# Attention on one core: the exponentials of four heads in one tile and one addition a step; copies and the next image's norm on ScalarE; the projection's matmuls together

## The chip, the cores and the metric

The kernel runs on one core of a Trainium2 chip. The metric is the device time of one execution in microseconds (us), given as the median of several runs, lowest and highest behind it. In the profiles PE is TensorE's matmuls, PEld its weight loads (they overlap PE), DVE is VectorE, ACT is ScalarE, POOL is GpSimd.

## The reference, cut to what matters

Everything is fp32; the input has four images of 256 channels and 48 by 48 pixels. Two layers follow one another. The first holds the part that the change touches:

```python
# layer 0: x = x + conv_layer(group_norm(x)), of which:
q, k, v = (qkv[:, :, :d], qkv[:, :, d:2 * d], qkv[:, :, 2 * d:])      # 8 heads of d = 32, N = 2304
attn = softmax(einsum('bhdn,bhdm->bhnm', q, k) * scale, axis=-1)
out = einsum('bhem,bhnm->bhen', v, attn).reshape(B, C, H, W)
out = einsum('oc,bchw->bohw', proj_w, out) + proj_b[None, :, None, None]
# layer 1: dynamic filters on group_norm(x), [cut]
```

## The kernel before

Each image goes through convolution and qkv, attention with projection, and the filter stage. Attention works in ten units for an image: two groups of four heads by five columns of queries (four of 512, one of 256). A unit has 18 steps, one for each 128 keys. `scores` of a step makes four products on TensorE and two exponentials on ScalarE, each over a pair of heads. `weigh` of the step before multiplies the exponentials by the values into `num` and lets VectorE add them into `acc`; the softmax sums come from `acc` over the partitions, with matmuls by ones, one for each head, at the end (`close`). Step 8 skips VectorE and goes straight into that sum.

```python
def scores(u, m):
    # [cut: four matmuls into ss[0], ss[1], two heads each]
    ps = []
    for pair in range(2):
        p = work0.tile([P, 2, QC], F32, tag=f"p{pair}", name=f"p_{b}_{u}_{m}_{pair}", bufs=3)
        nc.scalar.activation(p[:, :, :n], ss[pair][:, :, :n], AF.Exp, scale=QS)
        ps.append(p)
    return ps

def weigh(u, m, ps):
    # [cut: num, acc made at m == 0; four matmuls num[r] += vT, ps[j // 2][:, j % 2]]
    if m in DIRECT:                       # DIRECT = (8,)
        # [cut] sums(u, the four heads of ps, ...)
    elif m == 0:
        st["first"] = ps
    else:
        for pair in range(2):
            a = st["acc"][:, 2 * pair : 2 * pair + 2, :n]
            other = st["first"][pair][:, :, :n] if m == 1 else a
            nc.vector.tensor_tensor(a, other, ps[pair][:, :, :n], ALU.add)
    if m == NT - 1:
        st["out"] = work0.tile([P, QC], F32, tag="out", name=f"no_{b}_{u}")
        nc.vector.tensor_copy(st["out"][:, :n], st["num"][:, :n])

for i, (u, m) in enumerate(steps):
    ps = scores(u, m)
    if prev is not None:
        weigh(*steps[i - 1], prev)
    prev = ps
    if m == 2 and u:
        close(u - 1)                      # sums over partitions, 1/sum, ao = out * that
    if m == 6 and u % NH == 0:            # NH = 2: a finished column of 384 goes to the projection
        while (chunk + 1) * CH <= units[u][1]:
            project(chunk, ao, ps2(f"pp_{b}_{chunk}"))
            chunk += 1
    if m > 4 and u > 1 and spare:         # pieces of the next image's norm, one a step
        spare.pop(0)(ps_a)

def project(b, c, ao, pp, norm):
    for o in range(NH):
        for g in range(NH):
            nc.tensor.matmul(pp[:, o, :CH], wp[:, g, o * P : (o + 1) * P],
                             ao[:, g, c * CH : (c + 1) * CH], start=(g == 0), stop=(g == NH - 1))
        x1 = inside(t, o, c * R, R)
        nc.vector.scalar_tensor_tensor(out=x1, in0=rows_of(pp[:, o, :CH]), ...)   # + bias + x
        norm.part(o, c, x1)               # statistics, on VectorE
        # [cut: store of x1]
```

The projection thus alternates matmuls of one output half with VectorE's reading of that half, from one tile `pp` whose buffers are shared with the scores.

## Time and profile before

| | before |
|---|---|
| time, us | 3422.59 (3419.55 to 3422.88, three runs) |
| span of the profiled run, granted clock | 3419.3 us, 0.963 |
| PE, DVE, ACT busy, share of the span | 92%, 70%, 43% |
| attention, from first to last scores, images 0 to 3 | 414.3, 414.8, 418.4, 406.9 us |

The prediction shows the stages, the ring of the steps and the two places where TensorE waits for VectorE. Beside them, these are the groups of instructions that the change edits. A line reads: source line, engine, operation, output and inputs, their shapes, count, then busy time, mean ns of one, then idle time of the engine just before these instructions and what ended most of it.

```profile
L721 ACT ACTIVATE p<-se 128x1024 f32<-128x1024 f32 (+1 forms) x1440 | 1273.6, 937 | 377.2 <-PE se L709 341.0
L754 DVE TENSOR_TENSOR acc<-acc,p 128x1024 f32<-128x1024 f32 (+1 forms) x1200 | 1250.5, 1112 | 42.0 <-ACT p L721 41.1
```

Next the timeline, in which equal instructions that follow closely are one line: start, length, engine, line, tiles, count.

```profile
261.69 34.14 DVE L754 TENSOR_TENSOR acc<-acc,p 128x1024 f32<-128x1024 f32 x30
```

The table of waits (waiting engine and tile, waited-for engine and tile, then us in all, times, longest) also has:

```profile
PE num L737 <- DVE no L757: 35.4, 32, 3.3
PEld den L761 <- DVE acc L754: 1.8, 4, 0.5
```

The first is the copy that holds TensorE at the end of units. The second says that closing sums, which need the last addition, hardly wait.

### The profile page before, as it was taken

Reading aid. Unit: us, or ns where it says so; the run is one execution under the profiler, and the core shown is the slowest. Engines: PE = TensorE matmul, PEld = TensorE weight load, DVE = VectorE, ACT = ScalarE, POOL = GpSimd, SP = SyncE. Lnnn points to the kernel's source line nnn. Section 1 sums busy time; section 2 is a strip of 40 time slices with the busy share of each in tenths; the row PEclk is TensorE's granted clock in tenths of the full one; section 3 lists DMA queues with packets and bytes.
Section 4 is the critical chain, followed back from the end, with each engine's and each line's share of the span. In section 5 each row is a group of like instructions: output and inputs, shape, how many; then the busy total and the mean of one; then the engine's idle time right before and its main releaser. Section 6 shows DMA issues by size and latency. Waiting matters only on the chain. (4 is left out here: it accounts for less than half of the span.)

```text
span 3419.3 us, 45333 instructions
## 1 busy us (share of the span) xinstructions
PE 3158.2 (92%) x17814; PEld 1363.3 (40%) x17814; DVE 2377.3 (70%) x2837; ACT 1471.5 (43%) x1739; POOL 1041.5 (30%) x793
## 2 busy tenths in 40 slices
PE   7999999999989999999998999999998999987873
PEld 4542222445652222345563222245565222233442
DVE  2059899455659898836557899955555999876655
ACT  0067777300118777600024777730011887750002
POOL 0000000068770000037783000007786000007994
PEclk9999999999999999999999999999999999998876
DMA  3110000000002000000003000000000100022004
GB/s 119 29 27 6 6 10 6 15 24 5 10 14 52 6 6 10 11 28 10 5 10 61 6 6 10 6 6 5 5 10 16 23 6 6 10 81 100 10 5 176
DMA packets 70973, 81.52 MB, mean 24 GB/s; under 512 B 51280, under 2 KB 62048, under 8 KB 67680
## 3 DMA queue, kind: packets, MB, share of 16 engines
q1 hardware_dynamic: 69952, 73.15, 7.5%
q0 software_dynamic: 800, 5.41, 0.4%
q8 instruction: 141, 2.31, 0.3%
q14 instruction: 80, 0.66, 0.1%
HBM read 50.23 MB, written 28.31 MB: 23 GB/s over the span
## 5 line engine op out<-in xcount | busy, mean ns | idle before, releaser
L1060 POOL TENSOR_TENSOR cat<-cat,prod 128x768 f32<-128x768 f32 (+7 forms) x768 | 1034.1, 1352 | 2330.1 <-DVE prod L1058 2288.0
L721 ACT ACTIVATE p<-se 128x1024 f32<-128x1024 f32 (+1 forms) x1440 | 1273.6, 937 | 377.2 <-PE se L709 341.0
L754 DVE TENSOR_TENSOR acc<-acc,p 128x1024 f32<-128x1024 f32 (+1 forms) x1200 | 1250.5, 1112 | 42.0 <-ACT p L721 41.1
L709 PE MATMUL se<-q,k 32*128 32x512 f32 (+1 forms) x5760 | 830.5, 602 | 15.8 <-ACT p L721 12.6
L1058 DVE TENSOR_TENSOR prod<-wb,pad 128x768 f32<-128x768 f32 (+7 forms) x768 | 560.5, 750 | 404.4 <-PE wb L1035 369.8
L737 PE MATMUL num<-p,vT 128*32 128x512 f32 (+1 forms) x5760 | 716.6, 568 | 35.4 <-DVE no L757 35.4
L631 PE MATMUL pc<-pad,wc 128*128 128x384 f32 x1728 | 624.1, 494 | 2.3 <-issue 2.3
L1035 PE MATMUL wb<-w,pick 90*128 90x384 f32 (+3 forms) x888 | 478.7, 563 | 58.6 <-DVE prod L1058 52.2
L709 PEld LDWEIGHTS se<-q,k 32*128 32x128 f32 x5760 | 285.1, 184 | 565.2 <-issue 452.7
L631 PEld LDWEIGHTS pc<-pad,wc 128*128 128x128 f32 x1728 | 317.7, 191 | 219.1 <-issue 47.7
L990 PE MATMUL py<-cat,wsc 128*128 128x384 f32 x960 | 365.9, 511 | 16.7 <-POOL cat L1060 16.7
L737 PEld LDWEIGHTS num<-p,vT 128*32 128x32 f32 x5760 | 114.8, 108 | 529.5 <-issue 464.2
L640 ACT ACTIVATE hid<-pc,bn_t_f,bn_s_f 128x384 f32<-128x384 f32 x48 | 32.2, 672 | 614.5 <-PE pc L631 614.5
L1035 PEld LDWEIGHTS wb<-w,pick 90*128 90x128 f32 x888 | 172.3, 197 | 220.2 <-DVE prod L1058 101.6
L990 PEld LDWEIGHTS py<-cat,wsc 128*128 128x128 f32 x960 | 187.2, 200 | 127.4 <-POOL cat L1060 22.9
L875 PE MATMUL pg<-pad,wcat 128*45 128x384 f32 x864 | 173.1, 514 | 2.5 <-DVE pad L585 2.2
L1050 DVE TENSOR_TENSOR cat<-wb,pad 128x768 f32<-128x768 f32 x120 | 114.6, 955 | 86.9 <-PE wb L1035 86.3
L1005 ACT COPY y<-py 128x768 f32<-128x768 f32 x24 | 19.2, 799 | 317.4 <-PE py L990 317.4
L651 PE MATMUL pq<-hid,wqkv 128*128 128x384 f32 x384 | 135.0, 486 | 0.0
L679 DVE TENSOR_REDUCE qm<-q 128x1 f32<-128x2304 f32 x8 | 20.4, 2546 | 156.6 <-ACT q L658 156.5
L812 PE MATMUL pp<-ao,wp 128*128 128x384 f32 x192 | 82.2, 559 | 38.0 <-DVE pad L820 37.1
L754 DVE TENSOR_TENSOR acc<-p,p 128x1024 f32<-128x1024 f32 (+1 forms) x80 | 85.8, 1115 | 32.2 <-ACT p L721 32.2
(115 smaller groups left out, 1085.1 us busy)
## 6 DMA issues: line engine op xcount, KB each, us to landing
pad<-in_x SPq DMA_DIRECT2D x14, 1152.0 KB, 14.7
x_d<-pad SPq DMA_DIRECT2D x48, 192.0 KB, 2.5
y_d<-y SPq DMA_DIRECT2D x24, 384.0 KB, 2.7
xst<-in_x SPq DMA_DIRECT2D x18, 384.0 KB, 3.9
y<-y_d SPq DMA_DIRECT2D x3, 2304.0 KB, 19.6
out<-y SPq DMA_DIRECT2D x6, 1152.0 KB, 12.6
x<-x_d SPq DMA_DIRECT2D x2, 2304.0 KB, 24.2
x_first<-in_x SPq DMA_DIRECT2D x2, 1152.0 KB, 7.3
```

The source lines that it names most:

```text
L631: nc.tensor.matmul(pc[:, :CH], wc[:, i, k, o * P : (o + 1) * P], window(gn, i, c * R, k // 3 - 1, k % 3 - 1), start=(i == 0 and k == 0), s ...
L651: nc.tensor.matmul(pq[:, :CH], wqkv[:, i, s, g * P : (g + 1) * P], hid[:, i, cols], start=(i == 0), stop=(i == NH - 1),)
L709: nc.tensor.matmul(ss[j // 2][:, j % 2, :n], k_[r, g, m * P : (m + 1) * P], q[r, g, q0 : q0 + n], start=True, stop=True,)
L721: nc.scalar.activation(p[:, :, :n], ss[pair][:, :, :n], AF.Exp, scale=QS)
L737: nc.tensor.matmul(st["num"][r, :n], vT[:, m, g * P + j * D : g * P + (j + 1) * D], ps[j // 2][:, j % 2, :n], start=(m == 0), stop=(m == N ...
L754: nc.vector.tensor_tensor(a, other, ps[pair][:, :, :n], ALU.add)
L875: nc.tensor.matmul(pg[64 * s : 64 * s + NG, :CH], wcat[:, i, k, :], window(gn, i, (c + s) * R, k // 3 - 1, k % 3 - 1), start=(i == 0 and k ...
L990: nc.tensor.matmul(py[c][:, o, :CH], wsc[:, n * NH + i, o * P : (o + 1) * P], rhs(i), start=(n == 0 and i == 0), stop=(n == len(DILATIONS) ...
L1035: nc.tensor.matmul(pw[:, : nr * WW], pick[:, k : k + 1].to_broadcast([2 * NG, P]), w[:, l0 * WW : l1 * WW], start=True, stop=True,)
L1050: nc.vector.tensor_tensor(accv, wb, src, ALU.mult)
L1058: nc.vector.tensor_tensor(pv, wb, src, ALU.mult)
L1060: nc.gpsimd.tensor_tensor(dst, dst, pv, ALU.add)
```

## The change

The intent: fewer instructions on VectorE (one addition of 2048 elements a step instead of two of 1024), two kinds of work moved from VectorE to ScalarE (the copy of `num`, the normalising of the next image), and a projection whose eight matmuls run through before VectorE's reading is needed.

```diff
@@ Norm.finish
                 self.mean, self.rstd = mean, rstd
+                self.shift = small.tile([P, NH], F32, tag="gshift", name=f"gshift_{self.name}")
+                nc.vector.scalar_tensor_tensor(
+                    out=self.shift, in0=mean, scalar=-1.0, in1=rstd, op0=ALU.mult, op1=ALU.mult
+                )
@@ scores
-                ps = []
+                p = work0.tile([P, 4, QC], F32, tag="p", name=f"p_{b}_{u}_{m}", bufs=3)
                 for pair in range(2):
-                    p = work0.tile(
-                        [P, 2, QC], F32, tag=f"p{pair}", name=f"p_{b}_{u}_{m}_{pair}", bufs=3
-                    )
-                    nc.scalar.activation(p[:, :, :n], ss[pair][:, :, :n], AF.Exp, scale=QS)
-                    ps.append(p)
-                return ps
+                    nc.scalar.activation(
+                        p[:, 2 * pair : 2 * pair + 2, :n], ss[pair][:, :, :n], AF.Exp, scale=QS
+                    )
+                return p
@@ weigh (the matmuls and sums() take p[:, j] instead of ps[j // 2][:, j % 2]; cut)
-                    for pair in range(2):
-                        a = st["acc"][:, 2 * pair : 2 * pair + 2, :n]
-                        other = st["first"][pair][:, :, :n] if m == 1 else a
-                        nc.vector.tensor_tensor(a, other, ps[pair][:, :, :n], ALU.add)
+                    a = st["acc"][:, :, :n]
+                    other = st["first"][:, :, :n] if m == 1 else a
+                    nc.vector.tensor_tensor(a, other, p[:, :, :n], ALU.add)
                 if m == NT - 1:
                     st["out"] = work0.tile([P, QC], F32, tag="out", name=f"no_{b}_{u}")
-                    nc.vector.tensor_copy(st["out"][:, :n], st["num"][:, :n])
+                    nc.scalar.copy(st["out"][:, :n], st["num"][:, :n])
@@ project
                         stop=(g == NH - 1),
                     )
+            for o in range(NH):
                 x1 = inside(t, o, c * R, R)
@@ piece of the next image's norm
-                    return lambda ps_a: normalize(t, t, nn.mean, nn.rstd, h)
+                    return lambda ps_a: nc.scalar.activation(
+                        t, t, AF.Identity, bias=nn.shift[:, h : h + 1], scale=nn.rstd[:, h : h + 1]
+                    )
```

More of the change, by code (lines that the diff above doesn't have):

```diff
@@ L715, in scores, with weigh @@
                     )
-                ps = []
+                p = work0.tile([P, 4, QC], F32, tag="p", name=f"p_{b}_{u}_{m}", bufs=3)
                 for pair in range(2):
-                    p = work0.tile(
-                        [P, 2, QC], F32, tag=f"p{pair}", name=f"p_{b}_{u}_{m}_{pair}", bufs=3
-                    )
-                    nc.scalar.activation(p[:, :, :n], ss[pair][:, :, :n], AF.Exp, scale=QS)
-                    ps.append(p)
-                return ps
+                    nc.scalar.activation(
+                        p[:, 2 * pair : 2 * pair + 2, :n], ss[pair][:, :, :n], AF.Exp, scale=QS
+                    )
+                return p
             state = {}
-            def weigh(u, m, ps):
+            def weigh(u, m, p):
                 g, q0 = units[u]
@@ L739, in weigh @@
                         vT[:, m, g * P + j * D : g * P + (j + 1) * D],
-                        ps[j // 2][:, j % 2, :n],
+                        p[:, j, :n],
                         start=(m == 0),
@@ L746, in weigh @@
                         st["den"] = ps_a.tile([P, 512], F32, tag="den", name=f"den_{b}_{u}")
-                    sums(u, [p[:, jj, :n] for p in ps for jj in range(2)], m == DIRECT[0], False)
+                    sums(u, p[:, :, :n], m == DIRECT[0], False)
                 elif m == 0:
-                    st["first"] = ps
+                    st["first"] = p
                 else:
-                    for pair in range(2):
-                        a = st["acc"][:, 2 * pair : 2 * pair + 2, :n]
-                        other = st["first"][pair][:, :, :n] if m == 1 else a
-                        nc.vector.tensor_tensor(a, other, ps[pair][:, :, :n], ALU.add)
+                    a = st["acc"][:, :, :n]
+                    other = st["first"][:, :, :n] if m == 1 else a
+                    nc.vector.tensor_tensor(a, other, p[:, :, :n], ALU.add)
                 if m == NT - 1:
                     st["out"] = work0.tile([P, QC], F32, tag="out", name=f"no_{b}_{u}")
-                    nc.vector.tensor_copy(st["out"][:, :n], st["num"][:, :n])
+                    nc.scalar.copy(st["out"][:, :n], st["num"][:, :n])
             def sums(u, rhs, start, stop):
+                n = rhs.shape[2]
                 for j, r in enumerate(heads):
-                    nc.tensor.matmul(state[u]["den"][r, : rhs[j].shape[1]], ones, rhs[j],
+                    nc.tensor.matmul(state[u]["den"][r, :n], ones, rhs[:, j, :],
                                      start=start, stop=stop)
@@ L768, in close @@
                 st = state[u]
-                sums(u, [st["acc"][:, j, :n] for j in range(4)], False, True)
+                sums(u, st["acc"][:, :, :n], False, True)
                 t = work0.tile([P, QC], F32, tag="rden", name=f"rt_{b}_{u}", bufs=1)
```

## The prediction

> **What bounds the kernel now.** I read the page first (busy shares, then the costliest groups), then the busy time of each engine by stage, then the timeline of single steps, then the table of who waits for whom. The kernel has four images, each with an attention stage and a stage of dynamic filters. The change touches attention and the projection that hangs on it. Busy time by stage, first attention of images 0 to 3, then their filter stages; columns are the stretch, its length, then PE, PEld, DVE, ACT and POOL busy, granted clock, DMA share and GB/s:
>
> ```profile
> 212.80:629.70 416.90, 395.95 (x3078) 113.78 (x3079) 376.91 (x410) 321.19 (x364) 0.00 (x0) 0.98 0.03 6
> 1022.00:1441.50 419.50, 397.46 (x3089) 114.10 (x3086) 377.61 (x412) 321.12 (x363) 0.00 (x0) 0.98 0.09 18
> 1836.00:2258.50 422.50, 400.40 (x3085) 115.29 (x3080) 377.20 (x411) 321.20 (x363) 0.00 (x0) 0.98 0.09 18
> 2646.00:3057.00 411.00, 393.46 (x3078) 112.55 (x3072) 371.34 (x391) 319.74 (x361) 0.00 (x0) 0.99 0.06 13
> ```
>
> Attention is 1670 us of 3419, and no engine fills it alone: PE 95%, VectorE 90%, ScalarE 77%. That asks for the timeline. One attention is 10 units (two head groups by five query columns, the last of 256 instead of 512), each of 18 steps. Steady steps, then the end of unit 1, of image 0:
>
> ```profile
> 286.97 1.94 ACT L721 ACTIVATE p<-se 128x1024 f32<-128x1024 f32 x2 [0.19 <-PE se L709]
> 286.98 1.06 PE L737 MATMUL num<-p,vT 128*32 128x512 f32 x8
> ...
> 287.97 1.20 PE L709 MATMUL se<-q,k 32*128 32x512 f32 x8
> ...
> 289.10 1.06 PE L737 MATMUL num<-p,vT 128*32 128x512 f32 x8
> ...
> 289.15 1.94 ACT L721 ACTIVATE p<-se 128x1024 f32<-128x1024 f32 x2 [0.24 <-PE se L709]
> ...
> 295.58 1.94 ACT L721 ACTIVATE p<-se 128x1024 f32<-128x1024 f32 x2 [0.18 <-PE se L709]
> 295.75 0.68 DVE L757 COPY no<-num 128x512 f32<-128x512 f32 x1
> ...
> 296.49 1.07 PE L737 MATMUL num<-p,vT 128*32 128x512 f32 x8 [0.83 <-DVE no L757]
> ```
>
> The reader is to see a ring. Two exponentials take 1.94 us, 0.19 later the weighting matmuls run, 1.00 later the next scores, 1.17 later the exponentials of two steps on: 1.94 + 0.19 + 1.00 + 1.17 = 4.30 us for two steps, 2.15 each, repeated exactly (exponentials 286.97 to 288.91, weighting 289.10, as 286.98 to scores 287.97 to exponentials 289.15). VectorE is not in the ring: it adds without a pause from 261.69 to 295.8, 30 additions at 1.138, 2.28 us a step, so it falls behind by 0.12 a step and catches up at the step whose sums TensorE takes. Its lag costs only where something on PE waits behind it. There are two such places: the copy of the finished unit (above, PE idle 0.83), and the projection:
>
> ```profile
> 407.63 1.56 PE L812 MATMUL pp<-ao,wp 128*128 128x384 f32 x4
> 410.64 0.62 DVE L820 SCALAR_TENSOR_TENSOR pad<-pp,pbias,pad 128x384 f32<-128x384 f32 x1
> ...
> 411.31 1.56 PE L812 MATMUL pp<-ao,wp 128*128 128x384 f32 x4 [2.12 <-DVE pad L820]
> 412.79 0.31 PEld L709 LDWEIGHTS se<-q,k 32*128 32x128 f32 x8 [0.55 <-issue]
> ```
>
> The second half of the projection writes the tile that VectorE reads for the first half; VectorE gets there after four queued additions. PE stands from 407.63 to 412.79, 5.16 us, for matmuls worth 2.7. The wait table gives the totals (us in all, times, longest):
>
> ```profile
> PEld num L737 <- DVE no L757: 61.5, 36, 4.1
> PEld pp L812 <- DVE pad L820: 53.0, 24, 3.1
> ```
>
> **What the skill says.** ScalarE: Activation LUTs, section "What ACT_TABLE_LOAD costs": an ACTIVATE takes 186 ns + 0.833 ns an element, 93 more for each pointer operand, and neighbours overlap by about 93. For 1024 that is 1039; the trace has 1022 and two in 1.94. For the new normalising (384 elements, pointer bias and scale) it gives 692; the trace has 672 for the like-shaped relu at L640. VectorE: DVE Perf Modes, section on the TRN2 errata: an fp32 addition takes (N+151)/0.96 ns; 1224 for 1024, trace 1219; so 2291 for 2048, an estimate. TensorE: Matmul & The Clock Gate, Part 1: after an idle window of about 3.4 us PE runs at half rate for a like time. The trace agrees: after a wait of 3.28 us at 350.13 eight weighting matmuls take 1.94 instead of 1.06, and scores 2.09 instead of 1.14.
>
> **The change part by part.**
>
> *One addition a step.* Two of 1.138 become one of about 2.20 (the slope between the 687 ns of 512 and the 1219 of 1024 is 1.04 ns an element). It saves 0.07 us a step, and lag grows by 0.05 a step instead of 0.12. In the ring this is worth nothing. It costs a little at the end of an image, where the last addition starts only after both exponentials: about 0.5 us four times, -2. The exponentials three steps on now wait for the whole addition; after a unit's closing I count them starting 0.3 to 0.5 us after it, so no wait, but not by much.
>
> *Copy to ScalarE.* It stands behind the exponentials of the next unit's first step. At 295: those end at 295.39, the copy ends near 295.95 (the 128x512 copy at L676 took 586 ns), the weighting starts at 296.0 instead of 296.49, and the next exponentials are pushed by about 0.25. Gain 0.5. At boundaries where VectorE waited less (PE idle 0.54) the gain is 0.24; at the end of unit 3 (idle 1.63) and of unit 7 (1.52), 1.3. Summed over the nine boundaries of an image, without unit 2 where a next image is normalised: 4.7 us in images 0 to 2, 4.2 in the last. Total 18.
>
> *Projection's matmuls together.* Eight at 0.336 (conv matmuls of this shape run 20 in 6.72) are 2.7, so PE stands 2.8 instead of 5.16: 2.35 saved. VectorE then works off the tile in 0.62 + 0.65 + 0.62, ending at about 412.3; the scores that reuse its buffer come at 412.5, so no new wait. A double projection (unit 6, 10.4 us) saves 4.8. In unit 8, steps are half as long and the tile comes free late: 1.1. Per image 8.3 without unit 2, in the last image 10.7: 36. The sixth projection, outside, waits 0.71 four times: 3. Where PE went to half rate behind such a wait (units of 47.6 and 47.7 instead of 46.07 us) 3 more. Together 42.
>
> *Normalising on ScalarE.* It leaves VectorE, 12 pieces of 0.48 in each of images 0 to 2, and lands on an engine of the ring. A step then holds 2 x 0.92 + 0.58 = 2.4 to 2.5 on ScalarE instead of 2.15: +0.3 on ten steps of unit 2, a few of them hidden in the stall of the table loads, and two of unit 3: 3.2 an image lost. Against it: with the pieces VectorE needed 2.66 a step, its lag grew all through unit 2, the copy came 3.28 late, and PE ran at half rate after it. That end cost about 5.3 more than an even step, plus 1.1 in the next one. With the copy on ScalarE it costs 0.4. The projection of unit 2 saves only about 1.1, because the small matmul of the norm then waits on PE for VectorE's statistics, which still queue behind the projection's reading. So 6.4 + 1.1 - 3.2 - 0.4 = 3.9 an image, 12 in all.
>
> Sum: -2 + 18 + 42 + 12 = 70 us, from 3422.6 to about 3352; the half rate that I did not count (unit 2 of image 2 took 56.93, the others 53.64) puts it at **3350**.
>
> **Rivals.** (1) *VectorE was the bound.* Its 90% and the halved number of additions speak for it; then 0.07 us on 640 steps (45), 40 copies (25) and 36 norm pieces of 0.48 (17), 87 us of VectorE work, would come off beside the 42 of the projections, near 3295. Against it: the ring closes without VectorE, and its lag shows in no wait of the exponentials. (2) *ScalarE becomes the bound.* It gets 40 copies of 0.5 and 36 pieces of 0.58, 41 us, and it sits in the ring with only 0.2 us free a step. If all of it came on top, the gain falls to about 45: 3378. Against it: most copies fall where the ring was open anyway. (3) *The wait moves.* The merged tile comes free later and holds up exponentials, or the projection's tile holds up the scores. A miss of 0.2 us a step over half of 576 full steps would be 58 us, so about 3400. My margin is 0.3, so it is possible, not likely. (4) PE no longer falls to half rate at all in unit 2: 10 us better.
>
> **Range and chances.** Faster by over 2% means below about 3354 to 3355, 5 us from my number. Rivals 2 and 3 pull up, 1 and 4 down; my sum is uncertain by some 15 us. Range 3328 to 3374. Faster 0.61, within 2% 0.38, slower 0.01.
>
> **What would show it.** Ordinary steps still 2.15 us; additions of 2048 elements at 2.28 us each; PE's waits for the projection's VectorE reads gone from the 90 us of the table, and projections standing 2.8; waits for the copy about half a microsecond, now from ScalarE; unit 2 of images 0 to 2 near 50 us and an ordinary unit near 40.9 instead of 41.25. I am wrong if exponentials wait for additions, if steps with a normalising piece exceed 2.5 us, or if ordinary steps themselves get shorter.

## More of the kernel before

Thirty additions took 34.14 us without a gap. One lasts 1.218 us, so from start to start it is (34.14 − 1.22) / 29 = 1.135 us: neighbours overlap a little.

## The result, and the profile after

| | before | after |
|---|---|---|
| median, us | 3422.74 (3419.55 to 3423.08) | 3359.7 (3356.87 to 3362.08) |
| ratio | | 0.9818 (0.9801 to 0.9835) |
| profiled span, granted clock | 3419.3, 0.963 | 3357.6, 0.968 |
| DVE, ACT busy, us | 2377.3, 1471.5 | 2333.6, 1503.1 |
| attention, images 0 to 3, us | 414.3, 414.8, 418.4, 406.9 | 399.2, 402.4, 399.2, 393.0 |

A ratio is the mean time of one kernel's fast runs over that of the other's of the same rounds, so it is not quite the ratio of the medians; in brackets is its 95% interval. The kernel is 1.8% faster, which is "within 2%". The attention stages became 60.5 us shorter in sum, of 61.7 in the span. A second set of five runs of the unedited change (below as e9_after_again) gave 3366.01 us, ratio 0.9826.

The groups of the exponentials and additions after:

```profile
L722 ACT ACTIVATE p<-se 128x1024 f32<-128x1024 f32 (+1 forms) x1440 | 1275.1, 940 | 281.4 <-PE se L713 181.7
L755 DVE TENSOR_TENSOR acc<-acc,p 128x2048 f32<-128x2048 f32 (+1 forms) x600 | 1246.6, 2078 | 94.2 <-ACT p L722 40.6
```

Half as many additions are as much busy time, 1246.6 against 1250.5. The timeline shows that the time from start to start got longer:

```profile
262.67 35.83 DVE L755 TENSOR_TENSOR acc<-acc,p 128x2048 f32<-128x2048 f32 x15
...
269.92 1.94 ACT L722 ACTIVATE p<-se 128x1024 f32<-128x1024 f32 x2 [0.24 <-PE se L713]
...
272.24 1.94 ACT L722 ACTIVATE p<-se 128x1024 f32<-128x1024 f32 x2 [0.38 <-DVE acc L755]
...
274.63 1.94 ACT L722 ACTIVATE p<-se 128x1024 f32<-128x1024 f32 x2 [0.45 <-DVE acc L755]
```

One addition lasts 2.29 us, and fifteen take (35.83 − 2.29) / 14 = 2.396 us from start to start, where two halves took 2 × 1.135 = 2.27. The exponentials, which start every 2.15 us in a free ring, now wait for additions: at 272.24 and 274.63 they follow at 2.32 and 2.39 us, the additions' own pace.

The end of unit 1, where TensorE had waited 0.83 us for the copy:

```profile
296.44 0.59 ACT L758 COPY no<-num 128x512 f32<-128x512 f32 x1
...
297.09 1.06 PE L739 MATMUL num<-p,vT 128*32 128x512 f32 x8 [0.27 <-ACT no L758]
```

The copy now comes straight behind the exponentials, and TensorE waits 0.27 us. The projection in unit 2 of image 0 and the norm's small matmul behind it:

```profile
309.62 2.85 PE L814 MATMUL pp<-ao,wp 128*128 128x384 f32 x8
...
312.51 1.14 PE L713 MATMUL se<-q,k 32*128 32x512 f32 x8
313.09 0.61 DVE L823 SCALAR_TENSOR_TENSOR pad<-pp,pbias,pad 128x384 f32<-128x384 f32 x1
...
316.11 0.38 PE L617 MATMUL pv_n<-gd_n,gmat 128*128 128x2 f32 x2 [1.46 <-DVE gd_n L614]
```

Eight matmuls run in one piece and scores follow; VectorE's reading starts only after them. The price is the later statistics, for which TensorE stands 1.46 us. A step with a normalising piece on ScalarE:

```profile
329.91 1.96 ACT L722 ACTIVATE p<-se 128x1024 f32<-128x1024 f32 x2
331.72 0.74 ACT L1183 ACTIVATE pad<-pad,gshift_n,grstd_n 128x384 f32<-128x384 f32 x1
332.31 1.97 ACT L722 ACTIVATE p<-se 128x1024 f32<-128x1024 f32 x2
```

From 329.91 to 332.31 are 2.40 us: here ScalarE is the ring. And the waits of the kernel after that answer to those shown of before:

```profile
PEld num L739 <- ACT no L758: 34.2, 36, 1.1
...
ACT p L722 <- DVE acc L755: 19.6, 37, 1.3
...
PEld den L763 <- DVE acc L755: 13.0, 21, 1.4
...
PE num L739 <- ACT no L758: 7.4, 28, 0.3
```

The wait for the copy fell from 35.4 to 7.4 us on the matmuls and from 61.5 to 34.2 on their weight loads. The waits for the projection's reading (53.0 us on weight loads) are gone from the table. Two waits that name the addition are new or larger: 19.6 us of exponentials, 13.0 instead of 1.8 of the closing sums' weight loads. The table has two more new lines of exponentials, behind `pad` (36.3 us, 12 times) and `rc` (27.5 us, 28 times). They are new labels and not new waits: all 40 times the exponentials start 0.03 us after the end of their scores, as they mostly do where the table names the scores.

### The profile page after: what moved, and what is told of

Read it like the earlier page. It is cut to its first block, busy times and chain, and to the rows that moved or that the text cites. A ratio compares the mean times of both kernels' runs of the same rounds, so it can differ in the third digit from the quotient of the medians.

```text
span 3357.6 us, 43467 instructions
## 1 busy us (share of the span) xinstructions
PE 3146.6 (94%) x17814; PEld 1365.5 (41%) x17814; DVE 2333.6 (70%) x2129; ACT 1503.1 (45%) x1815; POOL 1040.6 (31%) x793
## 5 line engine op out<-in xcount | busy, mean ns | idle before, releaser
L755 DVE TENSOR_TENSOR acc<-acc,p 128x2048 f32<-128x2048 f32 (+1 forms) x600 | 1246.6, 2078 | 94.2 <-ACT p L722 40.6
L713 PE MATMUL se<-q,k 32*128 32x512 f32 (+1 forms) x5760 | 843.4, 601 | 13.0 <-ACT p L722 8.0
L713 PEld LDWEIGHTS se<-q,k 32*128 32x128 f32 x5760 | 294.4, 184 | 567.0 <-issue 468.8
L755 DVE TENSOR_TENSOR acc<-p,p 128x2048 f32<-128x2048 f32 (+1 forms) x40 | 83.1, 2078 | 47.2 <-ACT p L722 47.0
L888 ACT COPY lg<-pg 45x384 f32<-45x384 f32 x24 | 11.3, 473 | 205.1 <-PE pg L878 205.0
```

What stands on the lines that cost most here:

```text
L713: nc.tensor.matmul(ss[j // 2][:, j % 2, :n], k_[r, g, m * P : (m + 1) * P], q[r, g, q0 : q0 + n], start=True, stop=True,)
L755: nc.vector.tensor_tensor(a, other, p[:, :, :n], ALU.add)
```

## The experiments

The theory: the copy, the projection and the norm bring what was forecast, and the one long addition takes some of it back, because each addition reads what the one just before wrote. Rivals: the merged tile itself (its buffers come free later) costs, whatever the additions look like; or an addition of 2048 elements is simply that slow; or ScalarE's new work costs more than forecast. Twelve runs followed, e9 and e10 being repeats; all gave correct results.

| run | kernel | median, us | ratio to before (95%) |
|---|---|---|---|
| e1_halves | after, additions in two halves | 3341.07 | 0.9768 (0.9754 to 0.9781) |
| e2_two_acc | after, two accumulators in turn | 3377.77 | 0.9868 (0.9853 to 0.9883) |
| e3_one_add | before, merged tile and addition alone | 3519.87 | 1.0289 (1.0275 to 1.0303) |
| e4_projection | before, projection alone | 3372.64 | 0.9854 (0.9839 to 0.9869) |
| e5_copy | before, copy on ScalarE alone | 3394.44 | 0.9924 (0.991 to 0.9937) |
| e6_norm | before, norm on ScalarE alone | 3405.77 | 0.9956 (0.9942 to 0.9969) |
| e7_all_but_merge | before, those three together | 3346.58 | 0.9791 (0.9778 to 0.9804) |
| e8_norm_later | e1, norm begun a unit later | 3343.0 | 0.9778 (0.9764 to 0.9791) |
| e9_after_again | after, unedited | 3366.01 | 0.9826 (0.9811 to 0.9841) |
| e10_halves_again | e1 again, same chip as e9 | 3343.44 | 0.977 (0.9756 to 0.9783) |
| e11_norm_on_vector | e1, norm back on VectorE | 3347.61 | 0.9782 (0.9769 to 0.9796) |
| e12_two_lines | before, projection and copy alone | 3335.57 | 0.9752 (0.9738 to 0.9765) |

Where this section gives a part's worth in us, it is the ratio's distance from 1 times the 3421 us of before. The median of before was between 3420.3 and 3422.73.

### e1_halves: one tile, two additions

Everything of the change stays, the merged tile too; only the addition is split.

```diff
-                    a = st["acc"][:, :, :n]
-                    other = st["first"][:, :, :n] if m == 1 else a
-                    nc.vector.tensor_tensor(a, other, p[:, :, :n], ALU.add)
+                    for s in (slice(0, 2), slice(2, 4)):
+                        a = st["acc"][:, s, :n]
+                        other = st["first"][:, s, :n] if m == 1 else a
+                        nc.vector.tensor_tensor(a, other, p[:, s, :n], ALU.add)
```

> The changed kernel, but each addition of 2048 elements split into its two halves again (same tile of exponentials, everything else as changed). Theory A: one long addition starts only when the one before it has finished, because it adds into what that one wrote: 2.39 us from start to start in the changed kernel, against 2 x 1.138 = 2.28 when two halves alternate. Then here the additions go back to 1.14 us apart, the 19.6 us that exponentials wait for additions vanish, and the time falls from about 3360 to 3340 to 3352 us. Theory B: the additions are off the path either way, and the missing ten microseconds of the forecast are the half-rate clock of TensorE and sizes misjudged at unit ends: 3357 to 3362 us. A third view, that fewer and longer instructions are cheaper, expects this one to be slower than the changed kernel.

Measured: 3341.07 us (3340.58 to 3355.97). So it is the single addition that costs, and not, in the main, the merged tile (e10 and e7 below, which differ in the tile alone, are alike to 0.01 us in units 1 to 9 but for unit 8, where the tile costs 0.56 us). The five runs of this one kernel lie 15 us apart, which needed the repeat e10.

### e2_two_acc: long additions that don't depend on their neighbour

Still one addition of 2048 elements a step, but even and odd steps add into different accumulators, and `close` sums both. The direct step 8 is dropped to make the turns regular.

```diff
-DIRECT = (8,)
+DIRECT = ()
...
-                        acc=work0.tile([P, 4, QC], F32, tag="acc", name=f"acc_{b}_{u}"),
+                        acc=[
+                            work0.tile([P, 4, QC], F32, tag=f"acc{k}", name=f"acc{k}_{b}_{u}", bufs=1)
+                            for k in range(2)
+                        ],
...
-                    a = st["acc"][:, :, :n]
-                    other = st["first"][:, :, :n] if m == 1 else a
+                    a = st["acc"][0 if m == 1 else m % 2][:, :, :n]
+                    other = st["first"][:, :, :n] if m in (1, 3) else a
...
-                sums(u, st["acc"][:, :, :n], False, True)
+                st["den"] = ps_a.tile([P, 512], F32, tag="den", name=f"den_{b}_{u}")
+                for k in range(2):
+                    sums(u, st["acc"][k][:, :, :n], k == 0, k == 1)
```

> The changed kernel with two accumulators that take turns, so that no addition of 2048 elements reads what the one directly before it wrote. As many additions and as many matmuls of sums as in the changed kernel (the step that went to TensorE is added too, and the two accumulators are both summed at the end). Theory A (the wait for the addition just before): start to start 2.20 us in place of 2.39. Rival C (a long addition is slower for its own sake, through its size or through traffic in memory): still 2.39. The time matters less here: A expects 3340 to 3358 us, since the sums at the end come together, C some 3365 or more.

The timeline of e2, then its table of waits:

```profile
266.79 30.91 DVE L758 TENSOR_TENSOR acc<-acc,p 128x2048 f32<-128x2048 f32 x14
```

```profile
ACT p L722 <- DVE acc L758: 99.9, 64, 2.4
```

From start to start it is (30.91 − 2.29) / 13 = 2.20 us. That is the figure forecast for the long addition. The same operation of the same size takes 2.396 when it reads what the one before wrote, so the size is not the cause and the dependence is: 0.19 us an addition. The time missed, 3377.77 us instead of a gain: with one buffer for each accumulator the next unit's first additions wait for the closing sums, and exponentials wait 99.9 us in all. This run settles the mechanism; it is no better kernel.

### e3_one_add: the merge alone on the kernel before

The edit is the scores and weigh parts of the diff above, without the copy, the projection and the norm.

> The kernel before with one part of the change alone: one tile for four heads and one addition a step; the copy and the normalising stay on VectorE. Theory A: VectorE needs 2.39 us a step against 2.28, falls behind by 0.24 us a step, and the copy of the finished values, which stands behind the last addition, comes 1 to 2 us later, so a unit takes 42 to 43.5 us in place of 41.25: slower by 25 to 60 us, 3448 to 3483. Theory B: no change, 3420 to 3425. The intent of the change (halve the instructions): faster by up to 45 us.

Measured: 3519.87 us, 2.9% slower. I had not expected so much. The timeline at the end of unit 1, then the table of waits:

```profile
300.42 0.68 DVE L754 COPY no<-num 128x512 f32<-128x512 f32 x1
...
301.16 1.94 PE L735 MATMUL num<-p,vT 128*32 128x512 f32 x8 [2.33 <-DVE no L754]
...
303.02 1.79 PE L709 MATMUL se<-q,k 32*128 32x512 f32 x8
```

```profile
PEld num L735 <- DVE no L754: 109.4, 36, 4.4
PE num L735 <- DVE no L754: 83.0, 36, 3.5
```

The copy still stands in VectorE's queue, behind additions that lag by 0.24 us a step now (2.396 − 2.15) instead of 0.12 (2.27 − 2.15). TensorE waits 2.33 us instead of 0.83, and then the weighting matmuls take 1.94 instead of 1.06 us and the scores 1.79 instead of 1.14: the half rate of the prediction. Groups of eight 512-wide scores or weighting matmuls slower than 1.52 us number 60 here and 16 in the kernel before. The totals of the wait on the copy grew from 35.4 to 83.0 us and from 61.5 to 109.4. So the parts of the change aren't independent: the copy on ScalarE takes away the place where the merge does its largest damage.

### e4_projection, e5_copy, e6_norm: each other part alone

```diff
+            for o in range(NH):                       # e4: in project, before x1
```

```diff
-                    nc.vector.tensor_copy(st["out"][:, :n], st["num"][:, :n])
+                    nc.scalar.copy(st["out"][:, :n], st["num"][:, :n])          # e5
```

e6 is the first and last parts of the diff above (`self.shift` and `piece`).

> The kernel before with the projection's matmuls together, nothing else. By the forecast: 42 us less, 3380 us, with the projection of 8 matmuls taking 2.8 us and unit 4 about 43.7 us in place of 46.07. Rival: with the copy still on VectorE the time comes back as a longer wait at unit ends, since VectorE is 90% busy: then only 15 to 30 us less.

> The kernel before with the copy of the finished values on ScalarE, nothing else. By the forecast: 18 us less from the unit ends, and some of the late copy at the end of unit 2 (3.3 us of waiting in three images, then half rate) on top: 3385 to 3402 us; the wait of the weighting for the copy falls from 0.5 to 1.6 us to 0.27, and TensorE's waits at the projection stay. Rival (ScalarE sits in the ring, so the copy only changes place): 3415 to 3423.

> The kernel before with the next image's normalising on ScalarE, nothing else. By the forecast: steps with a piece go from 2.15 to 2.4 us on ScalarE, and the 3.3 us wait for the copy at the end of unit 2 shrinks below 1 us: 5 to 15 us less in all, 3407 to 3417. Rival (ScalarE is in the ring, so the pieces cost what they take): 5 to 15 us more, 3427 to 3437.

Measured: 50, 26 and 15 us, against 42, 18 and 12 of the forecast. The forecast of the copy left out unit 2, so more than 18 was to be expected. In e4 the wait for the copy is word for word that of before (35.4 us, 32 times, longest 3.3): that part doesn't reach it.

### e7_all_but_merge: the three together

Two tiles and two additions as before, with e4, e5 and e6 in one kernel.

> The change without its first part: two tiles of exponentials and two additions a step as before, with the projection together, the copy on ScalarE and the normalising on ScalarE. If only the waiting of one addition on the last hurts, and the shared tile is neutral, this equals the split-additions run: 3338 to 3346 us, 14 to 20 us faster than the changed kernel. If the shared tile itself helps or hurts (one release for four heads), it differs from that run by 5 us or more.

Measured: 3346.58 us, ratio 0.9791, a gain of 71.5 us where the three alone sum to 91. They overlap: each of them shortens the late end of unit 2 in images 0 to 2 (VectorE behind with pieces and projection reading), and that can be won only once. Units 2 and 3 of these images became 10.1 us shorter in e4, 19.3 in e5 and 14.6 in e6, 44.0 in sum, but 23.4 in e7; the difference of 20.6 is about the gap between 91 and 71.5. The same three terms were 42 + 18 + 12 = 72 in the forecast, which had counted unit 2 once.

### e8_norm_later: does the stall at the norm's start cost?

On top of e1, the norm begins in unit 3, away from the projection of unit 2.

```diff
-                if m > 4 and u > 1 and spare:
+                if m > 4 and u > 2 and spare:
```

> The changed kernel with split additions, and the next image's norm begun one unit later, in unit 3, which has no projection. The small matmul of the norm then no longer stands in TensorE behind VectorE's reading of the projection (1.46 us three times), and with it the half rate that follows: 3329 to 3338 us. If the stall of the two table loads is what counts, which stays, no gain: 3339 to 3343.

Measured: 3343.0 us, ratio 0.9778 against 0.9768 of e1: no gain. Units 2 and 3 of image 0 together take 90.87 us here and 90.94 in e1. In the timeline of e8, TensorE's wait at the small matmul fell from 1.34 us (e10) to 0.41, but the one before it, which the projection used to cover, now waits 1.21. The stall with the two table loads of the norm's square root (1.28 us each) moves along: no exponential runs from 357.76 to 361.03.

### e9_after_again and e10_halves_again: the size of the long addition's cost

Both on one chip, five runs each; e10 has the edit of e1.

> The changed kernel again, unedited, on the same chip as the two beside it, so that the cost of the long addition is read without a change of chip. From the first measurement: 3357 to 3362 us.

> The changed kernel with split additions again, on the same chip as the changed kernel. If the long addition explains the missing ten microseconds: 10 to 20 us under the changed kernel of this call (3340 to 3349), the profile's units 1, 4 and 8 shorter by 0.2, 0.3 and 0.6 us and no waits of exponentials for additions. If the first result was luck with the clock: within 5 us of it.

Measured: 3366.01 us (3355.81 to 3366.72), 4 us above what I expected, and 3343.44 us (3340.43 to 3344.19). The ratios 0.9826 and 0.977 have separate intervals; their quotient 1.0057 is some 19 us. All nine runs with the long addition (the change and e9) lie at 3355.81 or above, nine of the ten with halves (e1 and e10) at 3346.72 or below, and the tenth at 3355.97. The additions of e10 are 1.136 us apart again, (34.15 − 1.22) / 29:

```profile
261.81 34.15 DVE L756 TENSOR_TENSOR acc<-acc,p 128x1024 f32<-128x1024 f32 x30
```

In its table of waits the exponentials hardly wait for additions any more:

```profile
ACT p L722 <- DVE acc L756: 3.6, 6, 0.8
```

In the profile of the change it was 19.6 us, 37 times, and 20.3, 39 times, in e9. Ordinary units, timed from copy to copy of `num`, are 40.69 us instead of 40.87, unit 4 is 43.43 instead of 43.74, unit 8 is 28.74 instead of 29.35. Summed over the units, that is about 7 us. The two profiled spans are 26.0 us apart (3364.5 and 3338.5). Of the rest, 12 us lie in unit 0 of the four images and in unit 2 of images 1 and 2, where e9 has matmuls at half rate, and 7 outside attention, which I can't explain. Slow groups, counted as in e3, number 15 in e9's profile and none in e10's. But e1, the same program as e10, had 8 of them and a profiled span of 3354.0 us. Whether the long addition brings on half rate regularly, or e9 and e10 fell so by luck, stays open.

### e11_norm_on_vector: the place of the norm

e1 with the pieces of the norm back on VectorE.

```diff
-                    return lambda ps_a: nc.scalar.activation(
-                        t, t, AF.Identity, bias=nn.shift[:, h : h + 1], scale=nn.rstd[:, h : h + 1]
-                    )
+                    return lambda ps_a: normalize(t, t, nn.mean, nn.rstd, h)
```

> The changed kernel with split additions, and the normalising back on VectorE. Theory: moving it was worth something only because the copy stood behind VectorE's queue; with the copy on ScalarE, its pieces of 0.25 us a step on the ring cost more than VectorE's growing lag: units 2 and 3 together 89 to 90.5 us in place of 90.9, time 2 to 6 us under split additions alone. Rival (the forecast's view that VectorE's lag costs at the end of unit 2): exponentials wait for additions in unit 2, and 3 to 12 us more.

Measured: 3347.61 us, ratio 0.9782 (0.9769 to 0.9796) against 0.977 (0.9756 to 0.9783) of e10. The intervals overlap. I had expected units 2 and 3 at 89 to 90.5 us and a time 2 to 6 us under split additions alone. The units came so (89.08, 89.06 and 90.71 us in images 0 to 2, against 90.95 in e10), the time did not: this profile has 10 slow groups, that of e10 none. With the merged tile, where the norm runs isn't settled beyond 0.3%.

### e12_two_lines: projection and copy alone on the kernel before

The edits of e4 and e5 and nothing else.

> The kernel before with only two of the four parts: the projection's matmuls together and the copy on ScalarE. If the shared tile and the normalising on ScalarE add nothing beside these two, this is as fast as the best versions so far: 3339 to 3350 us. If the normalising on ScalarE is needed as well, its own gain of about 15 us is missing: 3353 to 3362.

Measured: 3335.57 us (3333.36 to 3344.83), ratio 0.9752. Its table of waits has the copy as in the full change:

```profile
PE num L737 <- ACT no L757: 7.4, 28, 0.3
```

Its interval is apart from that of the full change in e9 (0.9811 to 0.9841), so two edited lines beat the whole change by about 0.75% (0.9752 / 0.9826). It overlaps with that of e10. Against e7, which differs only in the norm, the ratios say some 13 us, measured on different chips. The profiles support a part of it: unit 2 takes 47.63 to 49.27 us in e12 and unit 3 40.68 to 40.85, where e7 has 49.66 and 41.28. That is 0.8, 2.6 and 2.6 us in the three images, 6 us in all; the rest isn't explained. A reading that fits: once the copy is off VectorE, no wait of TensorE within attention names the pieces in e12's table, while on ScalarE they stand in the ring.

## Why the prediction was right or wrong

The time, 3359.7 us, lies within the range, 10 us above the number. The larger chance, 0.61, was on faster by over 2%, and it came out 1.8%.

Units are timed from copy to copy of `num`.

- **The step that failed is "One addition a step".** The forecast had "one of about 2.20", a saving of 0.07 us a step, a lag growing "by 0.05 a step instead of 0.12", and −2 us in all. Measured is 2.396 from start to start, 0.13 more than the two halves, and a lag of 0.24 a step. The slope from which 2.20 was made came from additions of the kernel before that alternate between two halves, so each depends on the last but one. A single long addition depends on its neighbour, and e2 shows that this is the whole difference (2.20 without it). The cost was some 19 us between e9 and e10 instead of 2, of which about 7 can be read off unit by unit.
- **"So no wait, but not by much" failed with it.** That margin of 0.3 to 0.5 us, counted after a unit's closing, was used up by the growing lag: 37 waits, 19.6 us. Rival 3, a wait that moves, is what happened, but at 37 steps and not, as reckoned for 3400, with 0.2 us over half of all steps.
- **The ring was read rightly.** Ordinary units went from 41.25 to 40.87 us; "near 40.9" was forecast. That it fits so closely is in part luck: the copy alone brings 40.69 (e5), and the long addition, which was to cost nothing here, takes 0.18 back.
- **The projection held, a little under its worth.** A single one went from 5.16 to 2.78 us (2.8 forecast), the double one of unit 6 from 10.39 to 5.35. Alone it brought 50 us for 42.
- **The copy held.** TensorE waits 0.27 us for it; alone it brought 26 us, of which the forecast's 18 left out unit 2.
- **The norm held in its parts, not in its merit.** A step with a piece takes 2.41 us (2.4 to 2.5 forecast; the piece itself has a median of 734 ns alone between exponentials, where the forecast had used 672 to 692). Unit 2 of image 0 went from 53.64 to 49.71 (near 50 forecast), and the small matmul waits 1.46 us behind the projection's reading as described. But the norm was credited with curing the late copy at the end of unit 2, which the copy's own move cures: e12, without the norm's move, is faster than e7 with it.
- **The sum of the other three held, in part by luck.** Forecast 72 us, measured 71.5 in e7 (3346.58 us). But the projection and the copy alone bring 85 us (e12) where 42 and 18 were forecast, since the end of unit 2 was put down to the norm; and the norm, credited with 12, then loses 6 us by the profiles and some 13 by the ratios. The two errors cancel.
- **In unit 8** the forecast expected a gain of 1.1 us from the projection, and the change has a loss of 0.42 (28.93 to 29.35). The projection's gain came: 27.90 in e4. With copy and norm moved too it is 28.17 (e7), with the merged tile as well 28.74 (e10), and with the long addition 29.35. In this unit, whose steps are half as long, the tile takes back 0.56 us and the addition 0.62.
- **Rivals 1, 2 and 4.** VectorE was not the bound: a step of additions became 0.13 us longer, and ordinary units became shorter all the same. ScalarE didn't become the bound outside the steps with a piece. Half rate didn't vanish: 16 slow groups before and 16 after.

## What to carry to other kernels

Before merging two running additions into one, look at what each reads: two halves taking turns hide an addition's end behind the other half, and one long addition can't start before its predecessor is done. Measure from start to start, not by duration or by the number of instructions. An edit that takes TensorE's work out from behind a lagging engine's queue (two lines here) can be worth more than one that lightens that queue, and parts that cure the same late spot must not be summed.

## What the Trainium skill lacked or had wrong

- Perfetto Trace Analysis, section "Optimizing Scalar/DVE Operations", says that grouping into larger operations can improve throughput if the engine is saturated. In a running sum it made a step dearer: 2.396 us from start to start for one addition of 2048 elements, 2.27 for two of 1024 in turn. The page lacks that the end of an instruction overlaps with the next only where that doesn't depend on it (2.20 with two accumulators).
- VectorE: DVE Perf Modes, section "The DRAIN you can't avoid", says that a semaphore after each of a row of copies costs nothing extra. For fp32 additions that read the result of the one just before, the runs show 0.19 us each (2.396 against 2.20). No run here has dependent copies.
- TensorE: Matmul & The Clock Gate, Part 1, gives an idle window of about 3.4 us. Half rate showed here after the matmuls had waited only 2.33 us and their weight loads 3.15 (e3_one_add, 1.94 us for eight weighting matmuls instead of 1.06), and in the changed kernel after 1.46 us and 2.36 (eight scores at 316.42 took 1.90 us instead of 1.14). No page gives a length for such shorter waits. Two sets of runs of one kernel ran from 3340.58 to 3355.97 and from 3340.43 to 3344.19 us.
